# An adapter kernel's first microseconds: beta's rows by lane shuffles, the first batch of x loaded alone

## The chip, the cores and the metric

The kernel runs on one core of one Trainium2 chip. The core has five engines with an instruction queue each: TensorE (PE; its weight loads are listed apart as PEld), VectorE (DVE), ScalarE (ACT), GpSimd (POOL) and SyncE (SP), which here only issues DMAs. Sixteen DMA engines move data between the chip's main memory and the core. The metric is device microseconds of one execution; a kernel's time is the median of several runs.

## What is computed

128 batches, each of 128 tokens with 512 features (all float32), go through a low-rank adapter chosen by the batch's language (one of 9 ids, tables for 10), a residual, a layer norm with the language's gamma and beta, and a second residual. Cut to what matters:

```python
# x (128, 128, 512), ids (128,), W1 (10, 512, 128), W2 (10, 128, 512)
# b1 (10, 128); b2, gamma, beta (10, 512)
h = relu(einsum('bsh,bha->bsa', x, W1[ids]) + b1[ids][:, None, :])
y = x + einsum('bsa,bah->bsh', h, W2[ids]) + b2[ids][:, None, :]
mean = y.mean(-1, keepdims=True)
var = square(y - mean).mean(-1, keepdims=True)
out = x + (y - mean) * rsqrt(var + 1e-5) * gamma[ids][:, None, :] + beta[ids][:, None, :]
```

## The kernel before

One batch is one tile of 128 partitions (tokens) by 512 columns (features), 256 KB. Every instruction is chained to the one before it on its engine (`keep`, L49), so the order of the program is the order of each engine, written out by hand; the semaphores between engines, and those that say that a buffer is free again, are placed by the framework. It also gives each DMA one of eight semaphores in turn, whichever engine issues it, and a DMA waits until the one that had the same semaphore before it has landed.

What happens to a batch b in the steady state, one step of the loop at the end per batch (`i` is the batch that enters, `b = i - 3` the one whose residual is taken):

- SP loads x, four batches to a tile (`load_x`, L71; four such tiles), and stores results two batches at a time (`store`, L371).
- TensorE transposes x into PSUM (`transpose_x`, L235), multiplies by W1 (`down`, L258) and, two steps later, by W2 (`up`, L275): per step transposes of i, `down` of i-1, `up` of i-2. There is one PSUM buffer for transposes and there are five for `py`, the output of `up`.
- ScalarE copies the transposes to SBUF (`copy_xT`, L239), applies bias and relu (L266), squares (L315), and copies the batch's W1 to a fixed place (`stage_w1`, L226). The first nine batches have their W1 loaded directly (`load_first`, L154, five buffers `w1s`: from the sixth on a load waits until `down` has read an older one); batches 9 to 20 copy it from `w1e` (two loads, L162), later ones from `w1` (four loads, L103).
- GpSimd makes two tiles from x: `r` = x + b2 (`add_b2`, L245) and `o` = x + beta (`add_beta`, L252). Both read rows that were spread to all partitions, in `b2_b` and `beta_b`, at a place that a register picks by language; so the first reader waits for all ten rows. `o` is in a ring of five tiles of two batches each (pool `op`); its slot is free when the store of the pair five before has landed. `r` is in a ring of four.
- VectorE takes the residual y = py + r with its sum (L292), then the centred product with gamma (L358) and the final scale and add into `o` (L367), behind three small steps for the inverse root. For some batches b2 isn't added by GpSimd: VectorE adds it first (`vector_b2`, L285), or TensorE does by one more product into `py` (`b2_by_matmul`, L274).

Here r_b, o_b stand for GpSimd's two operations on batch b, and x_10 for the load of batches 10 and 11.

The start prepares the tables. The rows of beta, gamma and b2 (10 each) are loaded to 30 partitions of `rows`, and split by VectorE into three bfloat16 parts whose sum is the float32 row (L184 to L188). For each row one product with a column of `pick` (`spread`, L206) broadcasts it to all 128 partitions in PSUM, and VectorE (17 rows) or ScalarE (13) copies it to its table (L211, L209). These 30 rows are woven between the first work on batches 0 to 3. Nine and a half products of no use (`spin`, L484) precede all this on TensorE. SP issues in this order: ids, gamma, x of batches 0 and 1, part of W2, `w1s` 0 and 1, x of 2 and 3, `w1s` 2 and 3, the rest of W2, then x in pairs and `w1s` up to 8, both halves of `w1e`, x of 10 and 11, and from there the loop's loads and stores.

The last five batches have an order of their own (`tail`): GpSimd finishes batches 123 and 124 and a quarter of 125 (L415, L417), VectorE the rest; the last stores go out on SP's and ScalarE's queues (L420).

Of the kernel before, what the change touches and what calls it, by code (L numbers as in the profile page):

```python
# [8 lines left out]
FP = mybir.dt.float32  # L9
BF = mybir.dt.bfloat16  # L10
# [6 lines left out]
P = 128  # L17
# [5 lines left out]
U = 2  # L23
# [3 lines left out]
def cond_resid_kernel(ctx: ExitStack, tc: tile.TileContext, x, itok, W1, b1, W2, b2, gamma, beta, out):  # L27
# [60 lines left out]
        dst = xs[lo // G][:, lo % G : lo % G + hi - lo, :]  # L88
        keep(nc.sync.dma_start(out=dst, in_=x[lo:hi].rearrange("b s h -> s b h")))

    keep(nc.sync.dma_start(out=ids, in_=itok.rearrange("(o b) -> o b", o=1)))
# [4 lines left out]
    keep(nc.scalar.dma_start(out=b1r, in_=b1))  # L96

    warm = const.tile([P, 1], FP, name="warm")
    keep(nc.vector.memset(warm, 1.0))
    keep(nc.scalar.activation(warm, warm, AF.Abs_reciprocal_sqrt))  # L100
    def load_w1(k):
        keep(
            nc.sync.dma_start(out=w1[:, :, k, :], in_=W1[:, k * P : (k + 1) * P, :].rearrange("l p a -> p l a"))  # L103
        )

    ident = const.tile([P, P], FP, name="ident")
    make_identity(nc, ident)
    eps = const.tile([P, 1], FP, name="eps")
    nc.gpsimd.memset(eps, EPS)
    ones = const.tile([P, P], BF, name="ones")  # L110
    nc.gpsimd.memset(ones, 1.0)
# [10 lines left out]
    keep(nc.vector.tensor_scalar(pick[:, L : 2 * L], pick[:, L : 2 * L], -0.5, None, ALU.mult))  # L122

    lids, w1s = {}, {}

# [54 lines left out]
    load_early(5, L)  # L180
    load_part(2 * G + 2, 3 * G)

    left = rp.tile([P, H], FP, tag="r", name="left")
    keep(nc.vector.tensor_copy(parts[0:R, :], rows[0:R, :]))  # L184
    keep(nc.vector.tensor_tensor(left[32 : 32 + R, :], rows[0:R, :], parts[0:R, :], ALU.subtract))
    keep(nc.vector.tensor_copy(parts[32 : 32 + R, :], left[32 : 32 + R, :]))
    keep(nc.vector.tensor_tensor(left[64 : 64 + R, :], left[32 : 32 + R, :], parts[32 : 32 + R, :], ALU.subtract))
    keep(nc.vector.tensor_copy(parts[64 : 64 + R, :], left[64 : 64 + R, :]))  # L188

    b1T = const.tile([P, L], FP, name="b1T")  # L190

    def transpose_b1():
        b1p = p_h.tile([P, P], FP, tag="h", name="b1p")
        keep(nc.tensor.transpose(b1p[:, :L], b1r, ident[:L, :L]))
        keep(nc.vector.tensor_copy(b1T, b1p[:, :L]))


    beta_b = const.tile([P, L * H], FP, name="beta_b")
# [1 line left out]
    b2_b = const.tile([P, L * H], FP, name="b2_b")  # L200

    def spread(r, copier):
        t = (beta_b, gamma_b, b2_b)[r // L]
        row = p_y.tile([P, H], FP, tag="y", name=f"row_{r}")
        pick_r = pick[:, r : r + 1].to_broadcast([96, P])
        keep(nc.tensor.matmul(row, lhsT=pick_r, rhs=parts[:96, :], start=True, stop=True))  # L206
        dst = t[:, r % L * H : (r % L + 1) * H]
        if copier is nc.scalar:
            keep(nc.scalar.copy(dst, row))  # L209
        else:  # L210
            keep(nc.vector.tensor_copy(dst, row))  # L211
# [3 lines left out]


    def b2_by_matmul(b):
        return b in (5, B - 1)

    def b2_by_vector(b):  # L220
        return b < 4 or 8 <= b < B - 8 and (b % 4 == 1 if b < 24 else b % 16 in (1, 6, 11) or b % 32 == 30)

    def stage_w1(b):
        w1s[b] = wp.tile([P, KC, A], FP, tag="w1s", name=f"w1s_{b}")
# [43 lines left out]
    def up(b):  # L268
        v = lid(b, ET.PE)
        ys[b] = p_y.tile([P, H], FP, tag="y", name=f"py_{b}")  # L270
        m = b2_by_matmul(b)
        if m:
            pick_b = pick[:, bass.ds(v + 2 * L, 1)].to_broadcast([96, P])
            keep(nc.tensor.matmul(ys[b], lhsT=pick_b, rhs=parts[:96, :], start=True, stop=False))  # L274
        keep(nc.tensor.matmul(ys[b], lhsT=hT[b], rhs=w2[:, bass.ds(v * H, H)], start=not m, stop=True))  # L275
        del hT[b]
# [246 lines left out]
    for i in range(3, B + U):  # L523
        b = i - U - 1
        if b > G and b % G == 2 and b // G + 3 < NG:
            load_x(b // G + 3)
        if i == 5:
            load_x(3)
        if i in (8, 10, 12, 14):
            load_w1((i - 8) // 2)  # L530
        if i == 4:
            up(2)
        if i == 5:
            up(3)
# [12 lines left out]
        if i > 4 and on(i - 1):  # L547
            relu(i - 1)
        if i + 1 >= LATE and on(i + 1):
            stage_w1(i + 1)  # L550
        if i > 5 and on(i - U):
            up(i - U)


        g, half = divmod(b, 2)
        p = g - 1
        mine, old = 0 <= p < B // 2, 0 <= p - 1 < B // 2
        if b == E:
# [36 lines left out]

        for n, engine in ((i + 3, ET.Activation), (i - U + 3, ET.PE), (b + 1, ET.DVE), (b + 5, ET.Pool)):
            if on(n):
                lid(n, engine)

# [36 lines left out]
```

## Time and profile before

Three runs took 308.22, 308.50 and 308.82 us; the median is 308.5 us. The profiled execution has a span of 306.5 us from its first to its last instruction.

| | before |
|---|---|
| median of the runs | 308.5 us |
| span of the profiled execution | 306.5 us |
| busy: PE, DVE, ACT, POOL | 294.6, 295.9, 282.3, 283.9 us |
| granted TensorE clock, mean of the span | 0.989 |
| POOL: r L245, 97 operations; o L252, 128 operations | 135.7; 173.9 us |
| DVE: row copies L211 in the first 45 us, 17 of 0.684 to 0.685 us | 11.6 us |
| ACT: row copies L209, 13 of 0.59 us | 7.7 us |
| PE: picks L206, 30 | 7.6 us |
| first r on POOL starts; first o | 19.67; 10.98 us |
| transposes of batch 4 start; of batch 10 | 21.59; 33.80 us |
| DMA moved in the span | 77.85 MB |

Busy is the time in which an engine has an instruction under way; TensorE's products overlap, so that their means are longer than what one adds. In the waits, a line names the engine, what it was about to do, and what released it, with the total, the number of times and the longest in microseconds. In a timeline the columns are the start, the duration, the engine, line, operation and tiles. In the stretches, the busy times of PE, PEld, DVE, ACT and POOL follow the length of the stretch, each with its number of instructions, then the granted clock, the busy share of the DMA engines (packets overlap, so it can pass 1) and GB/s.

### The profile page before, as it was taken

To read this page: it belongs to the slowest core of one execution; us is meant where nothing else is said; L and a number is where in the kernel's file an instruction comes from. 1 tells how busy PE (TensorE), PEld (TensorE's weight loads), DVE (VectorE), ACT (ScalarE), POOL (GpSimd) and SP (SyncE) were. 2 spreads that over 40 slices of the span, in tenths; PEclk is the share of its full clock that TensorE was granted. 3 is DMA by queue.
4 is the path that set the end of the run, shared out by engine and by line. 5 is a ranking of instruction groups with operands and counts; after the bars stand their busy time and mean duration, and the time that the engine had idled before them with its cause. 6 is when DMAs were issued, how large, how long until landed. Compare 5 with 4: busy or idle time off the path is not lost. (4 is left out here: it accounts for less than half of the span.)

```text
span 306.5 us, 6981 instructions
## 1 busy us (share of the span) xinstructions
PE 294.6 (96%) x1835; PEld 220.0 (72%) x1835; DVE 295.9 (97%) x771; ACT 282.3 (92%) x777; POOL 283.9 (93%) x238
## 2 busy tenths in 40 slices
PE   8999999999999999999999999999999999999960
PEld 3748787777777777777777777777777777777730
DVE  6889999999999999999999999999999999999985
ACT  3858999999999999999999999999999999999981
POOL 1349899999999999999999999999999999999994
PEclk9999999999999999999999999999999999999995
DMA  6999999976678766766777666767776666773324
GB/s 231 379 390 388 373 371 354 387 231 240 221 255 276 250 202 241 226 257 219 259 276 243 213 209 238 265 224 260 275 238 206 226 231 242 246 266 137 135 109 171
DMA packets 43769, 77.85 MB, mean 254 GB/s; under 512 B 1961, under 2 KB 7348, under 8 KB 43730
## 3 DMA queue, kind: packets, MB, share of 16 engines
q1 hardware_dynamic: 43382, 76.84, 72.1%
q10 hardware_dynamic: 348, 0.57, 0.5%
q8 instruction: 15, 0.25, 0.3%
q14 instruction: 24, 0.20, 0.2%
HBM read 43.85 MB, written 33.55 MB: 253 GB/s over the span
## 5 line engine op out<-in xcount | busy, mean ns | idle before, releaser
L252 POOL TENSOR_TENSOR o<-x,beta_b 128x512 f32<-128x512 f32 x128 | 173.9, 1395 | 10.2 <-DVE beta_b L211 9.5
L245 POOL TENSOR_TENSOR r<-x,b_b 128x512 f32<-128x512 f32 x97 | 135.7, 1399 | 7.3 <-DVE b_b L211 6.2
L258 PE MATMUL ph<-xT,w1s 128*128 128x128 f32 x1024 | 135.4, 275 | 0.0
L275 PE MATMUL py<-w,hT 128*128 x256 | 131.2, 595 | 0.5 <-DVE b_b L211 0.5
L258 PEld LDWEIGHTS ph<-xT,w1s 128*128 128x128 f32 x1024 | 124.9, 192 | 1.0 <-ACT hT L266 0.5
L235 PEld LDWEIGHTS pxT<-ident,x 128*128 128x128 f32 x512 | 66.6, 151 | 65.3 <-issue 49.2
L358 DVE SCALAR_TENSOR_TENSOR py<-py,nmean,gamma_b 128x512 f32<-128x512 f32 x126 | 95.0, 754 | 0.9 <-ACT sq L399 0.8
L367 DVE SCALAR_TENSOR_TENSOR o<-py,rstd,o 128x512 f32<-128x512 f32 x122 | 91.2, 748 | 0.0
L315 ACT ACTIVATE sq<-py,sum 128x512 f32<-128x512 f32 x124 | 85.9, 693 | 2.8 <-DVE py L292 2.5
L235 PE MATMUL pxT<-ident,x 128*128 128x128 f32 x512 | 78.2, 276 | 0.0
L239 ACT COPY xT<-pxT 128x512 f32<-128x512 f32 x128 | 74.7, 584 | 3.5 <-PE pxT L235 3.5
L292 DVE SCALAR_TENSOR_TENSOR py<-py,r 128x512 f32<-128x512 f32 x97 | 67.0, 691 | 0.2
L226 ACT COPY w1s<-w 128x512 f32 x107 | 65.5, 612 | 0.0
L266 ACT ACTIVATE hT<-ph,b1T 128x128 f32<-128x128 f32 x128 | 46.9, 366 | 7.9 <-PE ph L258 2.6
L275 PEld LDWEIGHTS py<-w,hT 128*128 128x128 f32 x256 | 39.1, 192 | 2.9 <-issue 1.0
L315 ACT ACTIVATION_READ_ACCUMULATOR sq<-py,sum 128x1 f32 x124 | 25.0, 202 | 0.0
L292 DVE SCALAR_TENSOR_TENSOR py<-py,x 128x512 f32<-128x512 f32 x31 | 21.7, 699 | 0.4
L285 DVE TENSOR_TENSOR py<-py,b_b 128x512 f32<-128x512 f32 x29 | 20.2, 695 | 0.7 <-PE py L275 0.6
L325 ACT ACTIVATE root<-ssq,eps 128x2 f32<-128x2 f32 x62 | 16.4, 265 | 0.0
L292 DVE DVE_READ_ACCUMULATOR py<-py,r 128x1 f32 x97 | 13.7, 141 | 0.0
L306 ACT ACTIVATE nmean<-sum 128x2 f32<-128x2 f32 x62 | 12.3, 198 | 0.0
L329 DVE SCALAR_TENSOR_TENSOR part<-ssq,root 128x2 f32<-128x2 f32 x62 | 9.3, 151 | 0.2 <-ACT root L325 0.2
(55 smaller groups left out, 90.4 us busy)
## 6 DMA issues: line engine op xcount, KB each, us to landing
out_dram<-o SPq DMA_DIRECT2D x61, 512.0 KB, 3.4
x<-in_x_dram SPq DMA_DIRECT2D x29, 1024.0 KB, 6.2
x<-in_x_dram SPq DMA_DIRECT2D x6, 512.0 KB, 8.8
w1e<-in_L_cond_W_dram SPq DMA_DIRECT2D x2, 1280.0 KB, 12.3
w<-in_L_cond_W_dram SPq DMA_DIRECT2D x4, 640.0 KB, 8.1
w1s<-in_L_cond_W_dram SPq DMA_DIRECT2D x9, 256.0 KB, 8.4
w<-in_L_cond_W_dram SPq DMA_DIRECT2D x1, 1792.0 KB, 10.3
w<-in_L_cond_W_dram SPq DMA_DIRECT2D x1, 768.0 KB, 5.4
```

The costliest lines, as they stand in the source:

```text
L226: keep(nc.scalar.copy(w1s[b].rearrange("p k a -> p (k a)"), src))
L235: keep(nc.tensor.transpose(pxs[b][:, k, :], cols, ident))
L239: keep(nc.scalar.copy(xT[b], pxs.pop(b)))
L245: keep(nc.gpsimd.tensor_tensor(rs[b], xb(b), b2_b[:, bass.ds(v * H, H)], ALU.add))
L252: keep(nc.gpsimd.tensor_tensor(os[g][:, j, :], xb(b), beta_b[:, bass.ds(v * H, H)], ALU.add))
L258: nc.tensor.matmul(phs[b], lhsT=w1s[b][:, k, :], rhs=xT[b][:, k, :], start=(k == 0), stop=(k == KC - 1))
L266: keep(nc.scalar.activation(hT[b], phs.pop(b), AF.Relu, bias=b1T[:, bass.ds(lid(b, ET.Activation), 1)]))
L275: keep(nc.tensor.matmul(ys[b], lhsT=hT[b], rhs=w2[:, bass.ds(v * H, H)], start=not m, stop=True))
L292: nc.vector.scalar_tensor_tensor(ys[b], ys[b], 1.0, r, ALU.mult, ALU.add, accum_out=col(sums, b))
L315: nc.scalar.activation(sq, ys[b], AF.Square, bias=col(sums, b), scale=-float(H), accum_out=col(ssqs, b))
L358: nc.vector.scalar_tensor_tensor(ys[b], ys[b], col(nmeans, b), gamma_b[:, bass.ds(v * H, H)], ALU.add, ALU.mult)
L367: nc.vector.scalar_tensor_tensor(o, ys.pop(b), rstds[g][:, j : j + 1], o, ALU.mult, ALU.add)
```

## The change

- Rows of beta no longer go through TensorE. beta is loaded four times, to partitions 0, 32, 64 and 96 of a zeroed tile (four loads on ScalarE's queue), and VectorE writes each of the ten rows to all partitions by a lane shuffle within each group of 32 (`stream_shuffle`), ahead of its other row work.
- Only gamma and b2 (20 rows) are split and spread by TensorE. The upper halves of the float32 words are taken as the first and second bfloat16 part: two subtractions on VectorE, two copies on ScalarE (before: three casts and two subtractions on VectorE). ScalarE copies 15 of the 20 rows, and b1's transpose; VectorE copies the five odd rows of b2.
- x of batches 0 and 1 is loaded one batch at a time. The tile for the spin products is set first on GpSimd; there are eight of them.
- GpSimd makes o of batches 0 to 3 before its first r, and in the loop o runs with batch b+2 in place of b. b2 is added by TensorE for batches 0, 1 and 127 (before 5 and 127), by GpSimd for 2, 3 and 5.

```diff
-    keep(nc.scalar.dma_start(out=rows[0:L, :], in_=beta))
-    keep(nc.sync.dma_start(out=rows[L : 2 * L, :], in_=gamma))
-    keep(nc.scalar.dma_start(out=rows[2 * L : 3 * L, :], in_=b2))
-    load_part(0, 2)
+    beta_rows = rp.tile([P, H], FP, tag="r", name="beta_rows")
+    keep(nc.vector.memset(beta_rows, 0.0))
+    def load_beta(q, engine):
+        keep(engine.dma_start(out=beta_rows[32 * q : 32 * q + L, :], in_=beta))
+    keep(nc.scalar.dma_start(out=rows[0:L, :], in_=gamma))
+    keep(nc.sync.dma_start(out=rows[L : 2 * L, :], in_=b2))
+    load_beta(0, nc.scalar)
+    load_beta(1, nc.scalar)
+    load_part(0, 1)
+    load_beta(2, nc.scalar)
+    load_beta(3, nc.scalar)
+    load_part(1, 2)
...
-    R = 3 * L
+    R = 2 * L
...
-    keep(nc.vector.tensor_copy(parts[0:R, :], rows[0:R, :]))
-    keep(nc.vector.tensor_tensor(left[32 : 32 + R, :], rows[0:R, :], parts[0:R, :], ALU.subtract))
-    keep(nc.vector.tensor_copy(parts[32 : 32 + R, :], left[32 : 32 + R, :]))
-    keep(nc.vector.tensor_tensor(left[64 : 64 + R, :], left[32 : 32 + R, :], parts[32 : 32 + R, :], ALU.subtract))
-    keep(nc.vector.tensor_copy(parts[64 : 64 + R, :], left[64 : 64 + R, :]))
+    def upper(lo):
+        return rows[lo : lo + R, :].bitcast(BF)[:, 1 : 2 * H : 2]
+    keep(nc.vector.tensor_tensor(rows[32 : 32 + R, :], rows[0:R, :], upper(0), ALU.subtract))
+    keep(nc.scalar.copy(parts[0:R, :], upper(0)))
+    keep(nc.vector.tensor_tensor(parts[64 : 64 + R, :], rows[32 : 32 + R, :], upper(32), ALU.subtract))
+    keep(nc.scalar.copy(parts[32 : 32 + R, :], upper(32)))
...
     def b2_by_matmul(b):
-        return b in (5, B - 1)
+        return b in (0, 1, B - 1)
     def b2_by_vector(b):
-        return b < 4 or 8 <= b < B - 8 and (...)
+        return 8 <= b < B - 8 and (...)
...
-    spin(9, H)
-    spin(1, H // 2)
+    spin(8, H)
     def spread_turn(lo, hi):
         for r in range(lo, hi):
-            spread(r, nc.scalar if r % 7 in (1, 3, 5) else nc.vector)
+            spread(r, nc.vector if r >= L and r % 2 else nc.scalar)
...
+    for r in range(L):
+        keep(nc.vector.stream_shuffle(beta_b[:, r * H : (r + 1) * H], beta_rows, [r] * 32))
     x_turn(0)
     transpose_b1()
-    spread_turn(0, 4)
+    spread_turn(0, 5)
     x_turn(1)
-    spread_turn(4, 11)
+    spread_turn(5, 7)
     down(0)
     relu(0)
-    spread_turn(11, 15)
+    spread_turn(7, 10)
+    x_turn(2)
+    for n in range(4):
+        add_beta(n)
+    spread_turn(10, 12)
     down(1)
     relu(1)
-    x_turn(2)
-    spread_turn(15, 19)
+    spread_turn(12, 15)
     x_turn(3)
     down(2)
     relu(2)
-    spread_turn(19, 24)
+    spread_turn(15, 18)
     down(3)
     relu(3)
-    spread_turn(24, R)
+    spread_turn(18, R)
     up(0)
     up(1)
...
             add_b2(b + 2)
-            add_beta(b)
+            if 4 <= b + 2 <= E:
+                add_beta(b + 2)
```

E is 123; L, H and B are 10, 512 and 128. The line of beta's operation on GpSimd, L252 before, is L264 in the changed kernel, that of b2's is L257, and the row copies are L221 (ScalarE) and L223 (VectorE).

More of the change, by code (lines that the diff above doesn't have):

```diff
@@ L104, in load_w1 @@
         )
+    ones = const.tile([P, P], BF, name="ones")
+    nc.gpsimd.memset(ones, 1.0)
     ident = const.tile([P, P], FP, name="ident")
@@ L109, in cond_resid_kernel @@
     nc.gpsimd.memset(eps, EPS)
-    ones = const.tile([P, P], BF, name="ones")
-    nc.gpsimd.memset(ones, 1.0)
-    R = 3 * L
+    R = 2 * L
     parts = const.tile([P, H], BF, name="parts")
@@ L121, in cond_resid_kernel @@
     keep(nc.vector.tensor_tensor(pick, both, ident[:96, 64 : 64 + R], ALU.add))
-    keep(nc.vector.tensor_scalar(pick[:, L : 2 * L], pick[:, L : 2 * L], -0.5, None, ALU.mult))
+    keep(nc.vector.tensor_scalar(pick[:, 0:L], pick[:, 0:L], -0.5, None, ALU.mult))
     lids, w1s = {}, {}
@@ L194, in transpose_b1 @@
         keep(nc.tensor.transpose(b1p[:, :L], b1r, ident[:L, :L]))
-        keep(nc.vector.tensor_copy(b1T, b1p[:, :L]))
+        keep(nc.scalar.copy(b1T, b1p[:, :L]))
     beta_b = const.tile([P, L * H], FP, name="beta_b")
@@ L202, in spread @@
     def spread(r, copier):
-        t = (beta_b, gamma_b, b2_b)[r // L]
+        t = (gamma_b, b2_b)[r // L]
         row = p_y.tile([P, H], FP, tag="y", name=f"row_{r}")
@@ L217, in b2_by_matmul @@
     def b2_by_matmul(b):
-        return b in (5, B - 1)
+        return b in (0, 1, B - 1)
     def b2_by_vector(b):
-        return b < 4 or 8 <= b < B - 8 and (b % 4 == 1 if b < 24 else b % 16 in (1, 6, 11) or b % 32 == 30)
+        return 8 <= b < B - 8 and (b % 4 == 1 if b < 24 else b % 16 in (1, 6, 11) or b % 32 == 30)
     def stage_w1(b):
@@ L272, in up @@
         if m:
-            pick_b = pick[:, bass.ds(v + 2 * L, 1)].to_broadcast([96, P])
+            pick_b = pick[:, bass.ds(v + L, 1)].to_broadcast([96, P])
             keep(nc.tensor.matmul(ys[b], lhsT=pick_b, rhs=parts[:96, :], start=True, stop=False))
@@ L594, in cond_resid_kernel @@
             stage_w1(i + 1)
-        for n, engine in ((i + 3, ET.Activation), (i - U + 3, ET.PE), (b + 1, ET.DVE), (b + 5, ET.Pool)):
+        for n, engine in ((i + 3, ET.Activation), (i - U + 3, ET.PE), (b + 1, ET.DVE), (b + 6, ET.Pool)):
             if on(n):
```

5 lines of the change are left out of this document (2 added, 3 removed).

## The prediction

> **What bounds the kernel now.** The page gives four engines busy for 92 to 97% of the span, so I went by stages. First the stretches of five microseconds (span, busy time of each engine, granted clock, DMA share, GB/s):
>
> ```profile
> 5.00:10.00 5.00, 4.94 (x27) 3.08 (x26) 3.96 (x8) 3.37 (x7) 0.00 (x0) 1.00 1.03 386
> 15.00:20.00 5.00, 4.54 (x24) 2.58 (x24) 3.77 (x6) 3.33 (x7) 0.33 (x1) 1.00 1.05 393
> 30.00:35.00 5.00, 5.00 (x35) 4.06 (x35) 5.00 (x17) 4.66 (x13) 3.86 (x4) 1.00 1.05 387
> 60.00:65.00 5.00, 5.00 (x32) 3.66 (x31) 5.00 (x14) 4.91 (x15) 5.00 (x5) 1.00 0.76 283
> ```
>
> The start looks slack: VectorE, ScalarE and GpSimd idle. But the DMA engines are full from 5 us to past 60, at about 388 GB/s. Next the waits: of GpSimd between 19 and 64 us, then of TensorE's matmuls from 18 to 296 us.
>
> ```profile
> POOL r L245 <- DVE b_b L211: 6.2, 1, 6.2
> POOL r L245 <- DMA x<-in_x_dram: 1.1, 1, 1.1
> POOL o L252 <- DMA out_dram<-o: 0.5, 1, 0.5
> ```
> ```profile
> PE py L275 <- DVE b_b L211: 0.5, 1, 0.5
> ```
>
> After the start TensorE never waits (a batch takes it 2.22 us, later 2.19), and GpSimd waits three times in all. Which transfer the second wait is for, the one load of L89 issued at 19.1 us tells (batches 10 and 11); the third wait stands in GpSimd's timeline; the stores of 30 to 65 us give the time from issue to landing:
>
> ```profile
> L89 SPq DMA_DIRECT2D x<-in_x_dram x1: 2955/2955/2955, 19.1 to 19.1; - x1
> DMA to landing us min/median/max: 14.0/14.0/14.0
> ```
> ```profile
> 50.59 1.30 POOL L245 TENSOR_TENSOR r<-x,b_b 128x512 f32<-128x512 f32 x1
> 52.43 1.27 POOL L252 TENSOR_TENSOR o<-x,beta_b 128x512 f32<-128x512 f32 x1 [0.54 <-DMA out_dram<-o]
> 53.67 1.28 POOL L245 TENSOR_TENSOR r<-x,b_b 128x512 f32<-128x512 f32 x1
> ```
> ```profile
> DMA to landing us min/median/max: 5.0/8.0/8.9
> ```
>
> So x of batches 10 and 11 lands at 19.06 + 13.97 = 33.0 us, behind a full queue. At 52.43 GpSimd starts beta of batch 16 (o_16), in the pair's slot that the store of batches 6 and 7 has just left. From there it runs without a gap: 197 operations from 53.67 (r_19) to 296.56, 1.233 us each. The chain that ended last has the rest:
>
> ```profile
> 291.65 4.91 POOL o L252 x4
> 296.56 1.22 POOL n L415
> 301.69 0.42 POOLq L631
> 302.17 0.48 DVE o L424
> ```
>
> GpSimd and VectorE end within a microsecond of each other. The last store behind GpSimd (ScalarE's queue, issued 302.21) landed at 304.7, the last behind VectorE (issued 303.10) at 305.4; the span ends 1.1 later, 306.5. The median, 308.5, is 2.0 above that span; I add my difference to it.
>
> **The change, part by part.**
>
> *VectorE's start.* Out: 12 of 17 PSUM copies (0.684 each), three casts (0.415), b1T's copy (0.17), four b2 adds of batches 0 to 3 (0.70): 8.2 + 1.2 + 0.2 + 2.8 = 12.4 us. In: ten shuffles and a memset (128x256 took 0.27, so at most 0.54). No row has a shuffle; the nearest are the SBUF cast of 512 columns (0.415) and scalar_tensor_tensor (0.754), so ten cost 4.2 to 7.5; I take the fp32 subtraction's 0.682, 6.8. They wait for the fourth copy of beta. That load sits on ScalarE's queue and reuses the semaphore of gamma's load, so it starts when gamma has landed (rows had landed by 3.1) and lands near 4.7: beta_b is ready at 11.5 (8.9 to 12.2), against 10.98 now.
>
> The Trainium skill (VectorE: DVE Perf Modes, The perf-mode tier table) has STREAM_SHUFFLE in 1x mode only, about 2400 ns for 2048 columns. As an estimate from that page a quarter of it is 0.6 us, ten are 6.0, and beta_b would be ready at 10.7; no run here shows it yet.
>
> *ScalarE's start.* It issues six loads in place of three, and the last, b1r, waits until b2's rows have landed: the table load goes from 2.12 to about 3.4 (3.1 to 3.8) and, with its 1.28 and the warm-up's 0.20, ScalarE is free at 4.9. Then two casts (nearest rows 0.37 and 0.61; I take a copy's spacing, 1.07/2 = 0.54), 15 row copies and 4 xT copies at 0.54, four relus at 0.27, b1T at 0.17: 21 x 0.54 + 1.1 + 0.2 = 12.6, so b2_b is complete at 17.5 if ScalarE never starves and near 19.5 if it waits for each pick. Now VectorE completes it at 19.5. Everything in the start now hangs on ScalarE: xT of batch 0 queues behind the casts, so that x of batch 0 alone, landing at 4 to 5 us in place of 5.1, buys nothing, and neither do the 1.5 spin matmuls less.
>
> *TensorE's start.* Ten picks fewer (0.22 apart), two b2 picks in batches 0 and 1, one fewer in batch 5. Behind the last row come two picks and three products, 2 x 0.22 + 3 x 0.86 = 3.0, so the transposes of batch 4 start at 20.5 in place of 21.6; those of batch 10 would start at 33.80 - 1.1 - 0.2 = 32.5. But x_10 lands at 33.0: 33.15, a gain of 0.65 for TensorE and no more. ScalarE meets the same wall: w1e, whose second half was issued at 18.4 and took 13.3, lands at 31.7; the copy behind it starts at 32.20 now. The loads stand in the same order on SP's queue, beta adds 60 KB (0.16 us), so the wall stays.
>
> The Trainium skill (DMA: Bandwidth & Descriptors, Where 436 GB/s comes from) has HBM-bound transfers end at about 358 GB/s per core and the ports at 435. The trace's 388 lies between and decides; as an estimate by 435, the 11.6 MB that are through by 33.0 (the page's GB/s by slices) would be through some 3 us sooner.
>
> *GpSimd.* Three r more (batches 2, 3, 5), 3.7 us, all in its idle time before 19.7: beta of 0 to 3 ends at 11.5 + 4.9 = 16.4, ahead of r_2. The costly edit is the small one: beta runs two batches further ahead. os holds five pairs; o_2g reuses the slot of store g-5. Before, that store was issued at step 2g-6 of the loop and o_2g came at step 2g; now at step 2g-2, four batches (8.8 us) after the issue, while stores take 8.0 in the full stage. From r_2 at 17.5, 14 operations lead to o_10 at 34.8, but store 0 (issued at 30.1, some 7 us) holds it until 37; o_12 waits for store 1 (issued 34.18 plus 8.9: 43.1); o_16 for store 3, at 52.4 as now, since that store stands at the same place in a full queue. Before, r up to 18 were done at that moment; now r up to 16. Behind o_16 there is one operation more than before, and GpSimd has no gap to win it back: all ends 1.23 later. The lead of r over its residual, 5.0 at the least in midstream now (batch 90: r ends at 211.6, the residual starts at 216.6), shrinks by 1.23 + 2 x 1.23 + 0.65 = 4.35 and stays positive, so VectorE is not stopped.
>
> *Sum.* VectorE's end: 305.4 - 0.65 = 304.8. GpSimd's: 304.7 + 1.23 = 305.95, which now ends last, 0.5 later than 305.43. Span 307.0, median 308.5 + 0.5 = 309.0. Bounds: store 3 landing 0.6 sooner leaves the wait for store 1 as the next (o_16 at 51.75, -0.1 in all); a hole in the transfers of 0.5 makes it +1.0: 308.4 to 309.5.
>
> **The rivals.**
>
> *Only the wall counts.* If the o ring doesn't hold GpSimd back (stores landing a good 1.3 sooner), VectorE ends last: 308.5 - 0.65 = 307.85. For it: GpSimd waited for a store only once now. Against it: that wait was there with two batches more of room.
>
> *The start pays in full.* x_10 would have to land sooner. The DMA engines are at 0.99 of their time from 10 to 15 us against 1.05 later, as loads of w1s wait for products of batches 0 to 3 that now come sooner; then the gain is between what the transposes of batch 10 could gain (1.3, from 33.80 to 32.5) and the 2.0 of b2_b: 306.5 to 307.2. Against it: that slack is 5 x 0.06 = 0.3 us.
>
> *A hole at the start, slower.* Each load reuses the semaphore of the load eight before, and waits for its landing. With four more small loads the big second part of w2 no longer waits for x of batches 0 and 1 (landed 5.07, issue 6.04) but for w2's first part (landed 7.35): 1.4 us later, and the x and w1s loads behind it on SP too. 3.0 MB are issued by then (x of four batches, four w1s, w2's first part), 5 x 0.153 + 2.35 x 0.386 = 1.7 moved: 1.3 MB, 3.4 us of cover, against 1.4 of delay and the two that the first rows of all took from issue to use. From the point where the 16 engines share that cover so unevenly that it runs dry, the whole 1.4 passes to every landing: x_10 at 34.4, o_16 at 53.8, GpSimd 1.23 + 1.4 later, end 305.43 -> 307.3: 310.4.
>
> *The change doesn't do what it says*: at above (17.5 - 4.9 - 4.7) / 10 = 0.8 us a shuffle, o of batch 3 would end behind b2_b, and r_2 would wait for it. The wait at o_10 covers 2 us more, so this costs nothing until 1.0 us each; it goes into the upper end.
>
> **How the numbers follow.** A measurement of this kernel can tell about 0.2%, 0.6 us, from no change, and the forecast's +0.5 stands near that edge. Forecast case 0.55: 0.31 within, 0.24 slower. Only the wall 0.17: 0.09 faster, 0.08 within. Paid in full 0.11, faster. Hole (with dear shuffles) 0.17, slower. Together faster 0.20, same 0.39, slower 0.41. Predicted 309.0; range 307.4 to 310.6: it leaves out the start paid in full (0.11) and a few hundredths above the hole; the forecast's own is 308.4 to 309.5.
>
> **What would show it.** Right: L264 waiting for out_dram in several places from 35 to 57 us, o_16 near 52.4 with r_18 behind it; transposes of batch 10 at 33.1 to 33.3; ScalarE's last row copy at 17 to 19; shuffles of 0.4 to 0.75; ScalarE's last store landing after SP's. Wrong: DMA share well below 1 between 7 and 12 us (the hole); x_10 in before 32; no wait of L264 for stores, or GpSimd ending no later than now.

## The result, and the profile after

The changed kernel took 311.38 us (median of 4 runs, 310.84 to 313.54), the kernel before 308.66 beside it (308.22 to 308.85): 1.0102 of the time before, 95% interval 1.0066 to 1.0139. It is slower, and lies above the range of 307.4 to 310.6 us. The profiled execution (311.19 us) has a span of 309.1 us, 2.6 more than before.

First the stretches of the changed kernel that answer to those of before (length; busy time of PE, PEld, DVE, ACT, POOL; granted clock; DMA share; GB/s):

```profile
5.00:10.00 5.00, 1.51 (x6) 0.61 (x5) 1.55 (x6) 2.25 (x6) 0.00 (x0) 0.73 0.82 290
10.00:15.00 5.00, 5.00 (x22) 3.75 (x21) 4.96 (x15) 4.07 (x10) 0.00 (x0) 0.59 0.97 333
15.00:20.00 5.00, 5.00 (x38) 4.10 (x37) 2.27 (x4) 4.88 (x11) 4.96 (x4) 1.00 1.02 368
30.00:35.00 5.00, 5.00 (x35) 4.06 (x34) 4.99 (x14) 4.10 (x12) 5.00 (x5) 1.00 1.05 387
60.00:65.00 5.00, 5.00 (x33) 3.76 (x32) 5.00 (x14) 4.92 (x14) 5.00 (x5) 1.00 1.04 373
```

From 5 to 10 us everything is short of work at once: TensorE has 1.51 us of it where it had 4.94, and the DMA engines move 290 GB/s where they moved 386. In the next stretch TensorE is "busy" throughout, but at a clock of 0.59 (the trace has it at 0.50 from 7.27 to 14.10 us). The last row shows the other side: the queue that had thinned out to 283 GB/s by 60 us is still full at 373. Next the waits (engine and line, releaser, total, times, longest):

```profile
POOL o L264 <- DVE beta_b L513: 13.6, 1, 13.6
DVE beta_b L513 <- DMA w1s<-in_L_cond_W_dram: 4.2, 1, 4.2
PE b1p L206 <- DMA b1r<-in_L_cond_b_dram: 3.5, 1, 3.5
ACT L109 <- DMA beta_rows<-in_L_cond_beta_dram: 3.3, 1, 3.3
ACT b1T L207 <- PE b1p L206: 2.3, 1, 2.3
POOL r L257 <- DVE b_b L223: 1.8, 1, 1.8
POOL o L264 <- DMA out_dram<-o: 1.4, 2, 1.1
```

Two waits of about 4 us are new, and both are for small loads: TensorE waits for b1 (5 KB) and VectorE, ahead of its first shuffle, for the fourth copy of beta (20 KB; the row puts it down to a load of w1s that was landing at that moment, but a shuffle reads only `beta_rows`). ScalarE's 3.3 us are the issue of its six loads, done at 3.31. The chain of waits begins with b1, issued at 2.97 us and 5.61 us on its way; TensorE's timeline shows what that does:

```profile
2.97 5.61 DMA b1r<-in_L_cond_b_dram
```
```profile
4.42 0.72 PE L247 MATMUL pxT<-ident,x 128*128 128x128 f32 x4
8.62 0.27 PE L206 MATMUL b1p<-ident,b1r 10*128 10x10 f32 x1 [3.49 <-DMA b1r<-in_L_cond_b_dram]
8.83 2.31 PE L218 MATMUL row<-parts,pick 96*128 96x512 bf16 x5
10.94 1.06 PE L247 MATMUL pxT<-ident,x 128*128 128x128 f32 x4
```

x of batch 0 is there at 4.4 us, 1 us sooner than before. But the next product in TensorE's order transposes b1, so the picks wait behind it until 8.8, and then, at the lower clock, the five take 2.31 us, about 0.43 apart, in place of 0.22. Batch 4's transposes start at 23.79 (before 21.59), batch 10's at 35.77 (33.80). VectorE's side is as late: first shuffle 8.46, last done 14.96.

```profile
8.46 0.72 DVE L513 STREAM_SHUFFLE beta_b<-beta_rows 128x512 f32<-128x512 f32 x1
9.09 0.73 DVE L513 STREAM_SHUFFLE beta_b<-beta_rows 128x512 f32<-128x512 f32 x1
```

And GpSimd between 45 and 57 us, where o_12 and o_16 stand in the ring:

```profile
45.31 2.51 POOL L264 TENSOR_TENSOR o<-x,beta_b 128x512 f32<-128x512 f32 x2 [1.14 <-DMA out_dram<-o]
...
54.28 2.51 POOL L264 TENSOR_TENSOR o<-x,beta_b 128x512 f32<-128x512 f32 x2 [0.28 <-DMA out_dram<-o]
56.75 1.27 POOL L257 TENSOR_TENSOR r<-x,b_b 128x512 f32<-128x512 f32 x1
```

Where the 2.6 us of span come from: from batch 4 on TensorE waits no more. It is 2.20 late at batch 4 and 1.97 at batch 10, and VectorE's residual of batch 127 is 1.96 late (298.33, before 296.37). GpSimd's o of batch 127 starts 3.24 later (298.35 against 295.11), 1.28 more than that, one operation. So GpSimd's last store (ScalarE's queue) lands at 308.1, 0.7 behind the last of VectorE (307.4); before, it landed 0.7 ahead. About 2.0 us are the start, 0.65 the end.

### The profile page after: what moved, and what is told of

The parts are those of the page before. It is cut to its first block, busy times and chain, and to the rows that moved or that the text cites. A ratio compares the mean times of both kernels' runs of the same rounds, so it can differ in the third digit from the quotient of the medians.

```text
span 309.1 us, 6995 instructions
## 1 busy us (share of the span) xinstructions
PE 293.7 (95%) x1824; PEld 220.2 (71%) x1824; DVE 291.6 (94%) x772; ACT 283.8 (92%) x782; POOL 287.7 (93%) x241
## 4 chain that ended last, share of the span: by engine, by line
PE 89%; POOL 4%; DVE 2%; DMA 2%; issue 1%; POOLq 0%; ACTq 0%; DVEq 0%
PE ph L270 36%; PE py L287 34%; PE pxT L247 18%; PE row L218 2%; DMA b1r<-in_L_cond_b_dram 2%; POOL o L264 2%; POOL r L257 1%; POOL n L427 1%; DVE py L370 1%; POOL o L429 1%; DVE o L379 0%; POOLq L648 0%; DVE py L304 0%; ACTq L97 0%; DVE beta_rows L94 0%
## 5 line engine op out<-in xcount | busy, mean ns | idle before, releaser
L264 POOL TENSOR_TENSOR o<-x,beta_b 128x512 f32<-128x512 f32 x128 | 167.5, 1333 | 15.1 <-DVE beta_b L513 13.6
L257 POOL TENSOR_TENSOR r<-x,b_b 128x512 f32<-128x512 f32 x100 | 132.8, 1332 | 1.8 <-DVE b_b L223 1.8
L304 DVE SCALAR_TENSOR_TENSOR py<-py,r 128x512 f32<-128x512 f32 x100 | 69.1, 691 | 0.5
L304 DVE SCALAR_TENSOR_TENSOR py<-py,x 128x512 f32<-128x512 f32 x28 | 19.6, 699 | 1.1 <-PE py L287 0.4
L297 DVE TENSOR_TENSOR py<-py,b_b 128x512 f32<-128x512 f32 x25 | 17.3, 691 | 0.1
L318 ACT ACTIVATE nmean<-sum 128x2 f32<-128x2 f32 x62 | 12.3, 198 | 0.0
```

The lines of the kernel that those rows point to most:

```text
L257: keep(nc.gpsimd.tensor_tensor(rs[b], xb(b), b2_b[:, bass.ds(v * H, H)], ALU.add))
L264: keep(nc.gpsimd.tensor_tensor(os[g][:, j, :], xb(b), beta_b[:, bass.ds(v * H, H)], ALU.add))
L304: nc.vector.scalar_tensor_tensor(ys[b], ys[b], 1.0, r, ALU.mult, ALU.add, accum_out=col(sums, b))
```

## The experiments

All were timed beside runs of the kernel before, whose median was 308.54 to 308.74 us in each set. Ratios are to it, with a 95% interval; they are taken from all runs and differ a little from the quotient of the medians (1.0088 for the changed kernel).

| edit | us | ratio |
|---|---|---|
| changed kernel | 311.38 | 1.0102 (1.0066 to 1.0139) |
| b1 ahead of beta | 311.16 | 1.0074 (1.0057 to 1.0091) |
| o at batch b | 310.76 | 1.0058 (1.0041 to 1.0075) |
| x of 0 and 1 in one load | 310.53 | 1.0053 (1.0035 to 1.0071) |
| one copy of beta | 310.74 | 1.0068 (1.0045 to 1.0090) |
| b1 ahead, one load | 310.03 | 1.0059 (1.0043 to 1.0075) |
| b1 ahead, one load, o at b | 310.05 | 1.0037 (1.0022 to 1.0052) |
| beta copied on the chip | 310.56 | 1.0057 (1.0039 to 1.0076) |
| beta copied on the chip, one load | 310.38 | 1.0058 (1.0042 to 1.0074) |
| beta copied on the chip, one load, o at b | 309.40 | 1.0034 (1.0023 to 1.0045) |
| old loads, one load, o at b | 308.29 | 0.9990 (0.9977 to 1.0002) |
| old loads, one load, o two ahead | 309.16 | 1.0018 (1.0009 to 1.0027) |
| old loads, x split, o at b | 309.21 | 1.0028 (1.0013 to 1.0043) |
| kernel before, o two ahead | 309.36 | 1.0024 (1.0015 to 1.0034) |
| kernel before, x split | 309.54 | 1.0026 (1.0015 to 1.0037) |
| old loads, one load, o at b, b2 of 126 by TensorE | 307.61 | 0.9968 (0.9956 to 0.9980) |
| kernel before, b2 of 126 by TensorE | 307.88 | 0.9978 (0.9969 to 0.9988) |

### One part undone at a time

b1 loaded right behind gamma:

```diff
     keep(nc.scalar.dma_start(out=rows[0:L, :], in_=gamma))
     keep(nc.sync.dma_start(out=rows[L : 2 * L, :], in_=b2))
+    keep(nc.scalar.dma_start(out=b1r, in_=b1))
...
-    keep(nc.scalar.dma_start(out=b1r, in_=b1))
     keep(nc.scalar.activation(warm, warm, AF.Abs_reciprocal_sqrt))
```

> The changed kernel with b1's rows loaded ahead of beta's four copies on ScalarE's queue. If TensorE's late start alone costs the 2 us (it stood 3.5 us until b1's rows landed at 8.6, then ran at the lower clock): that wait goes, transposes of batch 4 start near 21 in place of 23.8, those of batch 10 near 33.5 in place of 35.8, median 2 us below the changed kernel's, about 309.4. If the hole in the transfers between 4.4 and 7.2 us costs them: x of batches 10 and 11 still lands near 35.1, transposes of batch 10 start at 35.2, and the median falls by 0.6 at most, to 310.8.

The wait for b1 is gone, the clock stays at 1.00, and xT of batch 4 is copied at 22.33, as before. Yet the time falls little, to neither of the two values expected, for two reasons that its waits and stretches show:

```profile
POOL o L264 <- DMA out_dram<-o: 4.1, 3, 1.7
PE ph L270 <- DMA w1s<-in_L_cond_W_dram: 1.7, 1, 1.7
DVE py L304 <- POOL r L257: 1.6, 3, 1.0
```
```profile
5.00:10.00 5.00, 2.76 (x16) 1.64 (x16) 2.37 (x8) 4.95 (x12) 0.00 (x0) 1.00 1.00 323
```

The transfers still run at 323 GB/s, so that now `w1s` of batch 0 is late, and batch 10, whose x comes later, starts at 34.34 (33.80 before) although batch 4 was on time. And once TensorE is on time, the ring stops GpSimd for 4.1 us: the lead of r over its residual falls to 0.25 us at batch 20, VectorE waits for r three times, and GpSimd's o of batch 127 starts at 298.6, no sooner than in the changed kernel (298.35).

o back at batch b in the loop:

```diff
-            if 4 <= b + 2 <= E:
-                add_beta(b + 2)
+            if 4 <= b:
+                add_beta(b)
```

> The changed kernel with beta's operation back at batch b of the loop (the first four stay ahead of the first r). If the ring of o tiles makes GpSimd end last (0.7 us behind SP's last store): no wait of o for a store between 35 and 60 us, GpSimd's last operation 1.2 sooner against TensorE's last product, the last store to land is SP's again, median 0.6 to 0.7 below the changed kernel's, about 310.7. If the end hangs on TensorE alone: within 0.2 of the changed kernel's. TensorE's own times don't move by either.

The time is what was expected. GpSimd no longer ends last: its o of batch 127 starts 1.08 us ahead of VectorE's residual, and r keeps some 5 us of lead in midstream. The profiled execution is the slowest of its runs (312.29): b1 landed at 9.7, and the start was later still.

x of batches 0 and 1 in one load:

```diff
-    load_part(0, 1)
+    load_part(0, 2)
...
-    load_part(1, 2)
```

> The changed kernel with x of batches 0 and 1 in one load again. If the split load makes half of the DMA engines stand between 4.4 and 7.2 us: the DMA share from 5 to 10 us goes from 0.82 back to 1.0, x of batches 10 and 11 lands near 33, and with TensorE's start no longer held by b1's rows the median falls by about 2, to 309.4. If beta's four copies make it: the share stays near 0.82, median within 0.5 of the changed kernel's.

The hole in the transfers is gone, though w2's second part was issued at 9.08 here, 3 us later than before:

```profile
5.00:10.00 5.00, 1.55 (x6) 1.04 (x7) 0.67 (x4) 1.78 (x4) 0.00 (x0) 1.00 1.03 376
```

TensorE waits 3.4 us for b1 all the same (busy 1.55 of 5), so the time lies between the two values expected. x of batches 10 and 11 is issued 3.1 us later than before (22.14) and lands at 34.01, 1.0 later, in spite of the full queue: the loads of w1s ahead of it wait for products that are late.

beta loaded once, to partitions 0 to 9, which leaves beta out of the result on the other 96 lanes (partitions 32 to 127):

```diff
     load_beta(0, nc.scalar)
-    load_beta(1, nc.scalar)
...
-    load_beta(2, nc.scalar)
-    load_beta(3, nc.scalar)
```

> The changed kernel with beta loaded once, to the first 32 partitions' group; on the other 96 partitions beta is zero in the output. If beta's copies cause both the late b1 rows and the hole: DMA share from 5 to 10 us near 1.0, b1's rows there by 5 us, transposes of batch 10 at 33.1 to 33.5, median 2 to 2.5 below the changed kernel's, 309 to 309.4. If the split x load makes the hole: share stays near 0.82 and x of batches 10 and 11 lands near 35, median 310.8.

No wait for b1 and shuffles from early on (DVE busy 5.00 us from 5 to 10); what is left is what the first run showed, w1s 2.4 us late at 315 GB/s and o waiting 3.5 us for stores, with GpSimd's o of batch 127 at 298.5. The time is the rival's: with one load of beta and x split the transfers stay slow, so the copies of beta don't make that hole. So undoing one part uncovers the next. Three costs were to be separated: late small loads, a slow queue, and the ring.

### Start mended, ring kept or undone

b1 ahead and x in one load, with o two ahead and with o at b (the edits above together):

> The changed kernel with b1 loaded ahead of beta and x of batches 0 and 1 in one load; o still runs two batches ahead. Theory (three costs that cover one another): both costs of the start are gone, so TensorE starts batch 4 by 22 us at full clock and the transfers of 5 to 10 us are back above 370 GB/s; what is left is the ring of o tiles, so GpSimd waits for stores of out_dram for over 2 us in all, ends after VectorE, and the time is 309.5 to 310.5 us. Rival (the late start is all of the loss): 308.0 to 308.7, GpSimd's last operations no later than VectorE's. Second rival (four copies of beta and the later second part of w2 keep the queue late whatever the split): x of batches 10 and 11 lands after 34.5 us again.

> As the run with b1 first and one load for x of batches 0 and 1, and o back at batch b as in the kernel before. Theory (three costs): no wait of o for stores above 1 us, VectorE ends last, 307.8 to 309.0 us, that is, within 0.3 us of the kernel before or a little faster; at least 0.7 us less than the same kernel with o two batches ahead. Rival (the ring costs nothing once the start is right): the two runs agree within 0.3 us. Second rival (shuffles and the late second part of w2 cost by themselves): 309.5 or more, with the transposes of batch 10 after 34.5 us.

The first is in time where the theory had it, with less of the ring than expected in it (o waits 1.7 us for stores, and GpSimd's last o starts 0.1 us after VectorE's residual) and a start that is still late (batch 4's xT is copied at 23.03). The second missed: 307.8 to 309.0 was expected, and it took 310.05. Its timeline of TensorE shows a wait that had been hidden until now:

```profile
12.89 0.38 PE L217 MATMUL row<-parts,pick 96*128 96x512 bf16 x1
15.57 1.01 PE L217 MATMUL row<-parts,pick 96*128 96x512 bf16 x2 [2.30 <-DVE b_b L222]
```

VectorE copies the odd rows of b2, the first of them behind all ten shuffles. These start at about 8.5, when the fourth beta copy lands, and end at 15, so the five PSUM tiles of the picks fill up and TensorE stands still for 2.3 us (1.5 in the other run of the pair); its clock is 0.66 in the next stretch. The late copies of beta therefore cost time in a second way, which b1's own wait had covered. That pair doesn't show the ring: the eight times of the second run fall in two groups, 308.79 to 309.37 and 310.05 to 310.25, and with the same start the profiled executions begin batch 4 at 22.30 and at 23.83.

### beta's three other copies made on the chip

beta loaded once, two copies by GpSimd and one by VectorE; then with x in one load; then with o at b as well:

```diff
+    load_beta(0, nc.scalar)
+    keep(nc.sync.dma_start(out=rows[L : 2 * L, :], in_=b2))
     keep(nc.scalar.dma_start(out=rows[0:L, :], in_=gamma))
-    keep(nc.sync.dma_start(out=rows[L : 2 * L, :], in_=b2))
-    load_beta(0, nc.scalar)
-    load_beta(1, nc.scalar)
...
+    for q in (1, 2):
+        keep(nc.gpsimd.tensor_copy(beta_rows[32 * q : 32 * q + L, :], beta_rows[0:L, :]))
...
+    keep(nc.vector.tensor_copy(beta_rows[96 : 96 + L, :], beta_rows[0:L, :]))
```

> The changed kernel with beta loaded once, ahead of gamma, and its three other copies made on the chip (two on GpSimd, one on VectorE); x of batches 0 and 1 still in two loads, o still two batches ahead. Theory (the late copies of beta hold the start, and the split load and the ring are costs of their own): shuffles start before 6 us in place of 8.5, beta_b is ready before 12.5 in place of 15.0, no wait of TensorE for b1 or for VectorE's row copies above 0.7 us; what stays is the split's lower transfer rate (below 345 GB/s from 5 to 10 us) and the ring (GpSimd ends last): 309.3 to 310.5 us. Rival (the loads alone were the loss): 307.8 to 308.6. Rival (the shuffles themselves cost, whenever they run): above 310.7.

> As the run with beta's copies made on the chip, and x of batches 0 and 1 in one load; the list of loads is now that of the kernel before. Theory: from 5 to 10 us over 370 GB/s, w2's second part issued near 6.0, x of batches 10 and 11 landed at 33.0 to 33.5 us as before; the ring is what is left: waits of o for stores over 1.5 us in all, GpSimd ends last, 308.9 to 309.7 us. Rival (only the wall counts): 307.7 to 308.3, VectorE ends last.

> As the run with beta's copies made on the chip and one load for x of batches 0 and 1, with o back at batch b: all three costs undone, the shuffles and ScalarE's copies kept. Theory: TensorE starts batch 4 at 20.0 to 21.5 and batch 10 at 33.1 to 33.8, VectorE ends last and no later than before, 307.6 to 308.6 us, at least 0.5 us below the same kernel with o two batches ahead. Rival (shuffles and ScalarE's load cost by themselves): 309 us or more with full transfers.

All three are slower than the theory had them, the first barely, the others by 0.7 and 0.8 us, and shuffles began at 8.06 in the third, hardly sooner. Its time is even that of its rival (the shuffles cost by themselves), which the next runs rule out. The cause lies in my own edit. The load of beta waits for the zeroing of its tile and is issued at 1.48, so gamma, behind it on the same queue, went out at 2.14, after x (1.50):

```profile
6.17 0.68 DVE L195 TENSOR_TENSOR rows<-rows 20x512 f32<-20x512 f32 x1 [3.33 <-DMA rows<-in_L_cond_gamma_dram]
```

gamma was 4 us on its way, where it had been in by 3.1. That is an unplanned repeat of the b1 case with another table: a 20 KB load issued behind x waits. The transfers were full in the third run (388 GB/s, w2's second part issued at 6.09 as before), so late small loads, gamma above all, cost 1.1 to 1.2 us here without any hole: 309.40 and 310.38 us, against 308.29 and 309.16 of the next two runs, which also take the copies of beta from another tile.

### The old list of loads, with the new start

beta goes to free rows of `rows`, first on ScalarE's queue as in the kernel before; gamma, b2, x of two batches and b1 stand at their old places. Three copies by GpSimd and one by VectorE put beta under the four groups of lanes. One run has o at batch b, one o two ahead, one o at b and x split:

```diff
+    def copy_beta(q, engine):
+        keep(engine.tensor_copy(beta_rows[32 * q : 32 * q + L, :], rows[64 : 64 + L, :]))
...
+    keep(nc.scalar.dma_start(out=rows[64 : 64 + L, :], in_=beta))
+    keep(nc.sync.dma_start(out=rows[0:L, :], in_=gamma))
+    keep(nc.scalar.dma_start(out=rows[L : 2 * L, :], in_=b2))
+    load_part(0, 2)
...
+    for q in range(3):
+        copy_beta(q, nc.gpsimd)
...
+    copy_beta(3, nc.vector)
```

> The loads stand exactly as in the kernel before (beta, gamma, b2, x of batches 0 and 1 in one load, b1); the four copies of beta for the shuffles are made on the chip (three on GpSimd, one on VectorE); o at batch b as before. Kept of the change: the shuffles, the split and the row copies by ScalarE, the order of the start, b2 by TensorE in batches 0 and 1. Theory (small loads issued behind the first x land some 4 us late, and that, the split load and the ring are all of the loss): beta, gamma and b2 are in by 3.5 us, shuffles run from about 5.5 to 12, TensorE has no wait above 0.7 us in the start, batch 4's transposes start at 20.5 to 21.8 in place of 21.6 before, 307.7 to 308.6 us. Rival (the new start itself is no shorter, because ScalarE's 15 row copies and its other work take it as long): the small loads land as before and batch 4's transposes start at 22.3 or later, 308.8 to 309.6 us.

> As the run with beta's copies made on the chip from a row load that stands first, but with o two batches ahead as in the change: this pair differs in the ring alone. Theory: GpSimd waits for stores for over 1.5 us in all, its last operations come after VectorE's, and the time is 0.6 to 1.3 us above the other run of the pair, 308.7 to 309.5 us. Rival (the ring is harmless): within 0.3 us of the other run.

> As the run with the old list of loads, beta copied on the chip and o at batch b, except that x of batches 0 and 1 comes in two loads as in the change: this pair differs in the split alone. Theory (the split by itself lowers the transfers at the start): 5 to 10 us moves under 345 GB/s in place of 392, x of batches 10 and 11 lands 0.5 to 1.5 us after 33.2 us, 308.8 to 309.6 us. Rival (the hole needs the added small loads): over 375 GB/s, within 0.3 us of the other run.

All three came out as the theory had them. With o at b, the first shuffle starts at 5.82, beta_b is ready at 12.3, the last row copy ends at 18.5, batch 4's transposes start at 20.62, and the transfers are full again:

```profile
5.00:10.00 5.00, 4.91 (x16) 2.93 (x17) 4.93 (x16) 3.67 (x8) 0.00 (x0) 1.00 1.04 392
```

From the timelines of that kernel, first VectorE's first shuffle, then TensorE's transposes of batch 4 and those of batch 10, which come at 33.29, at the wall:

```profile
5.82 0.72 DVE L512 STREAM_SHUFFLE beta_b<-beta_rows 128x512 f32<-128x512 f32 x1
```
```profile
20.62 0.63 PE L246 MATMUL pxT<-ident,x 128*128 128x128 f32 x4
...
33.29 0.72 PE L246 MATMUL pxT<-ident,x 128*128 128x128 f32 x4 [0.53 <-ACT hT L277]
```

The 1.0 us that batch 4 gains (20.62 against 21.59) has shrunk to 0.5 by batch 10. With o two ahead the same start pays 0.87 us for the ring, in its waits:

```profile
POOL o L263 <- DMA out_dram<-o: 4.0, 3, 1.9
```

With x split, the time is 0.92 us above the unsplit run. The first row is its stretch, the next that of the kernel before with nothing but the split:

```profile
5.00:10.00 5.00, 3.03 (x18) 1.82 (x17) 4.93 (x16) 4.38 (x10) 0.00 (x0) 1.00 0.94 335
```
```profile
5.00:10.00 5.00, 4.79 (x26) 2.79 (x25) 4.37 (x9) 3.66 (x7) 0.00 (x0) 1.00 0.94 327
```

How the rate reaches the time stands in the split run's transposes of batches 4 and 10: batch 4 starts as in the unsplit run (20.55 against 20.62), batch 10 is 1.35 later (34.64 against 33.29), since x_10 lands at 34.50 in place of 33.16.

```profile
20.55 0.64 PE L247 MATMUL pxT<-ident,x 128*128 128x128 f32 x4
...
34.64 0.72 PE L247 MATMUL pxT<-ident,x 128*128 128x128 f32 x4 [1.93 <-ACT hT L278]
```

### Single costs put into the kernel before

o two batches ahead, and x of batches 0 and 1 in two loads with b1 between them:

```diff
+            if b == 0:
+                for n in range(4):
+                    add_beta(n)
             add_b2(b + 2)
-            add_beta(b)
+            if 4 <= b + 2 <= E:
+                add_beta(b + 2)
...
```
```diff
-    load_part(0, 2)
+    load_part(0, 1)
     keep(nc.scalar.dma_start(out=b1r, in_=b1))
+    load_part(1, 2)
```

> The kernel before with one edit: o of batches 0 to 3 ahead of the first r, then o two batches ahead. Theory (ring): GpSimd waits for stores at o_10, o_12 and o_16, stands one operation (1.23 us) later to its end (beta of batch 127 ends at 296.3 in place of 295.1), ScalarE's last store lands last, 309.2 to 309.8 us. Rival (the ring counts only where the start is late): waits of o for stores under 0.7 us in all and 308.4 to 309.0 us.

> The kernel before with one edit: x of batches 0 and 1 in two loads in place of one. Theory (the split lowers what the queue moves at the start): 5 to 10 us moves 300 to 340 GB/s in place of 386, x of batches 10 and 11 lands about 1 us later than 33.0 us, 309.2 to 310.2 us. Rival (only the added small loads and the later second part of w2 make the hole): above 370 GB/s and 308.4 to 309.0 us.

Both cost what was expected, 0.6 and 0.8 us: o_12 waited 0.99 us and o_16 0.57 us for stores, and the beta operation of batch 127 began at 296.88 (before 295.11); with the split, w2's first part landed at 8.8 us (7.35 before). The profiled execution of the split is one of its shortest (308.66 us, the median is 309.54) and starts batch 10 only 0.24 later than before (34.04): it shows the lower rate, and the cost is shown by the medians.

### A version that beats both, and its control

b2 of batch 126 by TensorE's extra product in place of GpSimd, in the run with the old loads, one load of x and o at b, and in the kernel before (there 5 stands for 0 and 1):

```diff
-        return b in (0, 1, B - 1)
+        return b in (0, 1, B - 2, B - 1)
```

> As the run with the old list of loads, beta copied on the chip, x of batches 0 and 1 in one load and o at batch b (308.3 us, GpSimd's last store landing at 305.7 and VectorE's at 305.15), with b2 of batch 126 added by TensorE's extra product in place of GpSimd. Theory: GpSimd's end comes about 1.2 us sooner, VectorE ends last, so the time falls by what GpSimd was behind, 0.3 to 0.6 us, to 307.6 to 308.1 us, below the kernel before (308.5). Rival (the wall and the runs' spread decide): 308.2 to 308.5, no difference from the other run.

> The kernel before with one edit: b2 of batch 126 added by TensorE in place of GpSimd. Theory (GpSimd's last store lands 0.7 us ahead of VectorE's there, so taking work from GpSimd gives nothing without the earlier start): 308.3 to 308.8 us, no difference from the kernel before; so the 1.0 us that the repaired start gains with the same edit needs both. Rival (the edit at the end is all of that gain): 307.5 to 308.0.

The first is the fastest kernel of the study, 307.61 us, 0.32% (0.20 to 0.44) below the kernel before. The control says that most of it is not the changed start: the same edit gives the kernel before 0.22% (0.12 to 0.31). I had expected nothing there, since in the profiled execution of before GpSimd's store lands 0.7 us ahead of VectorE's. In the control's profile TensorE and VectorE happen to run 0.40 to 0.44 us sooner than in that of before, from batch 4 on, where the two programs are still the same, and GpSimd 0.6 later; with one more operation of 1.24 GpSimd's store would have landed there at about 304.27 + 1.24 = 305.5, behind VectorE's 304.99. So which engine ends last in the kernel before may differ from execution to execution; that is argued from this one trace and wasn't tried further. Between the two best kernels the intervals overlap: a gain of the mended start by itself is not shown.

## Why the prediction was wrong, point by point

**The start: the step that failed.** "That load sits on ScalarE's queue and reuses the semaphore of gamma's load, so it starts when gamma has landed (rows had landed by 3.1) and lands near 4.7." Starting was right (issued 2.6 us), landing was not: 8.4. I had priced the issue of three more small loads on ScalarE's queue, in the table load's 3.4 us (measured 3.34), but gave their transfers the time of loads that went out ahead of x. b1 I priced only as an instruction in ScalarE's way; that TensorE's order has b1's transpose ahead of all picks stood in the code, in `transpose_b1` between `x_turn(0)` and `spread_turn`, and I named nobody who waits for it. Every load of up to 20 KB issued by 1.4 us was in by some 3.2 us in the kernel before and in the runs with its list of loads; gamma issued at 2.14 came at 6.2, the fourth beta, issued at 2.6, at 8.4, b1 issued at 2.97 at 8.6. What b1's late place costs by itself on top of a mended start was not run.

**The terms behind it were nearly right.** A shuffle takes 0.72 to 0.77 and the next follows after 0.64, so ten take 6.5 us against my 6.8. ScalarE was free at 4.84 (I had 4.9); its casts took 0.60 and 0.62 (0.54) and a relu 0.37 (0.27), so that sum was some 0.5 us short. With the loads in time (the run with the old loads, one load of x and o at b), b2_b is complete at 18.5 (I had 17.5 to 19.5), batch 4's transposes start at 20.62 (20.5), batch 10's at 33.29 (33.15), and the time is 308.29, 0.44 above the rival "Only the wall counts" (307.85), which is less than a measurement can tell. Batch 4 at 20.62 is luck in part: the same start with o two ahead came to 19.82, because TensorE had its full clock sooner (last section). ScalarE's chain was sized rightly within 1 us; it was the data that came late.

The Trainium skill (VectorE: DVE Perf Modes, The perf-mode tier table) has 2400 ns for a shuffle of 2048 columns, a quarter of which, 0.6 us, was the estimate; the spacing of 0.64 us agrees with it.

**"The wall stays" failed too.** "The loads stand in the same order on SP's queue, beta adds 60 KB (0.16 us), so the wall stays." x_10 landed at 35.15, 2.1 later, w1e's second half at 33.81. I had counted bytes and order, not the rate at which the same bytes move. Between 5 and 10 us the changed kernel moves 290 GB/s with x split and 376 with x in one load; splitting lowers the kernel before from 386 to 327 with nothing else changed, and all runs with one load move 360 to 398. A late TensorE moves the wall too (34.01 in the run with x in one load). In the changed kernel itself the wall does not yet bind, since batch 10's transposes start 0.6 after x_10 has landed; it does once b1 is in time. The queue was also not at 388 GB/s all the way to 60 us, as I read it, but at 338 to 370 from 35 to 50; nothing hangs on that.

**The rival "A hole at the start" had the right sign and the wrong cause.** Its chance (0.17) was too low and its 310.4 us one microsecond short, and the hole came sooner than the 7 to 12 us at which I looked for it. It had the hole come from the late second part of w2. In the run with x in one load this part is issued at 9.08 us, 3 us later than before, and the stretch moves 376 GB/s; in the kernel before with x split it is issued at 6.86, and the stretch moves 327. The cover of 1.3 MB lasts.

**The ring was right, in mechanism and nearly in size.** One operation later to the end (1.28 of GpSimd's 3.24), o_16 behind store 3 with r_18 behind it, ScalarE's last store landing last. Against the kernel before I had +0.5 us for it, and the kernel before with it alone takes 0.62 more; on top of the start's gain I had 309.0 - 307.85 = 1.15, and the pairs that differ in o alone give 0.87 and 0.98 us. (In the pair with b1 ahead the medians agree within 0.02 us, and the ratios differ by 0.0022.) One thing I excluded came true elsewhere: r's lead "stays positive", yet it fell to 0.25 us at batch 20 in the run with b1 first, and VectorE waited.

**How it sums.** Put on top of the run with the old loads (0.9990), the ring adds 0.0028, the split 0.0038, and four beta loads with b1 ahead 0.0047 (1.0037 in the run with b1 ahead, one load and o at b); b1's own place behind them isn't in that. Together that is 1.0103, the changed kernel's 1.0102. That it comes out so closely is luck: the changed kernel's interval is wide, and in medians the same sum is 308.29 + 0.87 + 0.92 + 1.76 = 311.84 us against 311.38. The costs needn't add: with one undone, another takes its place, as the first four runs show.

**The base.** I took it from one execution that VectorE ends last by 0.7 us in the kernel before. The control suggests that this margin doesn't hold from run to run; then a cost on either engine counts in part.

## What to carry to other kernels

A small load was priced here by when it was issued against the big ones, not by its size: ask for each which product waits for it in program order, and put it ahead of the bulk or make copies on the chip. Bytes and order of a full queue do not fix when the last of them lands; compare the GB/s of each stretch once a load is split. And when two costs lie behind one another, undoing one shows little: build the version with all undone, and add them back singly.

## What the hardware showed unexpectedly

- After a 256 KB load of x at the head of the queue the 16 DMA engines are busy only 0.42 to 0.54 of the time from 4.75 to 6.25 us of the changed kernel (taken by half microseconds; 0.89 to 1.05 in the kernel before, with its 512 KB load), though later loads are already issued. In the kernel before with the split alone it is 0.56 to 0.69; in the run with the old loads and x split the hole comes later, 0.61 and 0.65 from 6.25 to 7.25. What these engines wait for, no run here shows.
- TensorE's first microseconds have two paces. The five first picks take 1.25 us in some kernels (0.22 apart) and 2.31 in others (0.43), the transposes of one batch 0.63 to 0.75 or 1.06 to 1.10. A clock of 1.00 in a stretch does not tell them apart, since the stretches count time for which the trace has no clock entry as 1.00. The trace's first entry, of full clock, begins at 10.24 us in the run with the old loads, one load and o at b, whose picks until then are 0.43 apart, and at 4.71 in the same with o two ahead, whose picks are 0.22 apart from the first one, at 5.83. All eighteen traces agree: the slow pace lies ahead of the first entry or inside one of 0.50, the fast one behind. The later full clock costs that start 0.8 us (batch 4's transposes at 20.62 and 19.82), which the wall then hides. In the run with x in one load the first entry begins at 13.66, in the run with o at b at 16.51, so a late clock is a part of their late starts. What sets the moment, no run here shows.
- Behind some waits the granted clock falls to half: from 7.27 to 14.10 us in the changed kernel (TensorE idle from 5.14 to 8.62), and from 15.15 to 18.56 in the run with b1 ahead, one load and o at b (idle from 13.27 to 15.57). An idle time of 1.5 us in the other run of that pair brought no fall.
